# Down projection: residual additions and stores by pairs of tiles, and the last tile's in two halves on two queues

## The chip, the cores and the metric

The kernel runs on one core of one Trainium2 chip. The metric is the device time of one execution in microseconds (us), as the median over several runs; it holds everything from the launch on the core to its end. A profile is taken of one further execution: its span goes from the first to the last instruction, its own device time is a little longer. PE is TensorE (PEld its weight loads), DVE is VectorE, ACT ScalarE, POOL GpSimd, SP SyncE; a "q" behind the name means the engine's instruction queue, which issues transfers (DMA) and waits.

## The reference, cut to what matters

The input is 4 x 512 tokens of 512 features. A layer norm is followed by two branches, a long convolution of the S4 kind and a gated feed-forward layer whose weights are stored as 4-bit codes with scales; both are added to the input.

```python
x = L0_attn_u                                   # (4, 512, 512)
xn = _layernorm(x, axis=-1)
x = x + _L0_attn_ref(xn, ...) + _L0_ffn_ref(xn, ...)

def _L0_ffn_ref(x, gate_q, gate_absmax, up_q, up_absmax, down_q, down_absmax):
    Wg = dequant_nf4(gate_q, gate_absmax, (M, HD))   # M = 1792, HD = 512
    Wu = dequant_nf4(up_q, up_absmax, (M, HD))
    Wd = dequant_nf4(down_q, down_absmax, (HD, M))
    g = jnp.einsum('bsh,mh->bsm', x, Wg)
    u = jnp.einsum('bsh,mh->bsm', x, Wu)
    h = jax.nn.silu(g) * u
    return jnp.einsum('bsm,hm->bsh', h, Wd)
```

The change touches the last step: the product of `h` with `Wd` (called Down here), and the addition of `x` plus the convolution's result to it.

## The kernel before

The 2048 tokens are worked on as four blocks (`tb` = 0 to 3) of 512, each block as four tiles (`j` = 0 to 3) of 128 tokens. The 1792 hidden features are 14 tiles of 128, or 7 pairs (`p`). Every product runs in fp32r in three passes ("parts"): each operand is split into three tensors, and three matmuls replace one.

There are four stages. First a head, whose order is written out by hand (`HEAD`) and fixed for ACT, DVE, PE and SP; it normalises and transposes the input and computes the first hidden tiles. Then the hidden tiles follow one by one (`hidden`, L472): PE multiplies (L449), ACT takes the silu (L465), DVE multiplies by the up product (L469) and SP stores `h` to device memory (L470). Between them lie the S4 kernel's computation and, for each block, the convolution (`conv`, L479 to L494), which adds `x` and stores the sum `xr` to `res_dram`. Last comes Down, one block after the other (`down`, L497 to L522), from 360 us on.

In Down, for each block:

- Two PSUM tiles of two banks each, `pj[0]` and `pj[1]`, hold the four tiles' sums in blocks 0 to 2 (`po[0]` and `po[1]` are the two banks of `pj[0]`). In block 3 each of the four sums has a two-bank tile of its own and uses the first bank (L500). PSUM holds four such two-bank tiles in all (`bufs=4`), so blocks 0 and 2 use the same two, block 1 the other two, and block 3 all four.
- POOL's queue loads the residual sum into `xr` (L505; the trace calls this tile `xo`). There are two such buffers, so a block's load waits until the stores of two blocks before have left the buffer.
- For each pair `p`, SP loads `h` (L508, tile `hr`, three buffers), ACT and DVE split it into three parts (L143, L145, L147; tile `hp`, four buffers), and PE runs for each tile `j` six matmuls (two hidden tiles times three parts) of 512 columns (L514): 24 for a pair, 168 for a block, 672 in all. The down weights stay in `wdt`.
- After a tile's last matmul (`p` = 6), DVE adds the PSUM sum times a constant to the residual, in place in `xr` (L521), and SP stores the tile's 128 rows of 512 numbers to `out` (L522), 256 KB each.

Outside the head a scheduler of the framework sets the order on each engine: it takes instructions in the order in which they were written, but lets a later one go ahead of one that would have to wait by its own reckoning. The framework also sets all semaphores. It tells apart which part of a tile in SBUF an instruction reads or writes; the trace of before shows that this doesn't always hold for the two banks of a PSUM tile. Each transfer issued by SP or ACT takes the next of eight completion counters, and at the very end SP waits on all of these in a fixed order, before a barrier of all engines closes the program.

Of the kernel before, what the change touches and what calls it, by code (L numbers as in the profile page):

```python
# [12 lines left out]
ALU = mybir.AluOpType  # L13
# [3 lines left out]
P = 128  # L17
NTOK = 2048
HD = 512
# [3 lines left out]
NTB = NTOK // 512  # L23
# [3 lines left out]
NPR = NMT // 2  # L27
# [23 lines left out]
OUT = LAM + 1.0  # L51
# [45 lines left out]
def layernorm_s4_nf4_glu_kernel(  # L97
# [17 lines left out]
    nc = tc.nc  # L115
    V, S, G, T = nc.vector, nc.scalar, nc.gpsimd, nc.tensor
# [5 lines left out]
    def bank2(name):  # L122
        return psum.tile([P, 2, 512], F32, tag="ps", name=name)
# [16 lines left out]
    def split(dst, src, ks=range(3)):  # L140
        for k in ks:
            if k == 0:
                S.activation(dst[0], src, AF.Copy, scale=TRIM)  # L143
            elif k == 1:
                V.tensor_tensor(dst[1], src, f(dst[0]), ALU.subtract)  # L145
            else:
                V.scalar_tensor_tensor(dst[2], f(dst[1]), -LAM, f(dst[0]), ALU.mult, ALU.add)  # L147
# [13 lines left out]
    def rows(ap, tb):  # L161
        return ap[bass.ts(tb, 512), :].rearrange("(j p) h -> p j h", p=P)
# [331 lines left out]
        nc.sync.dma_start(res_dram[tb], xr)  # L494


    def down(tb, wd):  # L497

        if tb == NTB - 1:
            po = [bank2(f"po{tb}_{j}")[:, 0, :] for j in range(4)]  # L500
        else:
            pj = [bank2(f"po{tb}_{jj}") for jj in range(2)]
            po = [pj[j // 2][:, j % 2, :] for j in range(4)]
        xr = work.tile([P, 4, HD], F32, tag="xt", name=f"xo{tb}")
        nc.gpsimd.dma_start(xr, res_dram[tb])  # L505
        for p in range(NPR):
            hr = work.tile([P, 2, 512], F32, tag="q", name=f"hr{tb}_{p}", bufs=3)
            nc.sync.dma_start(hr, h_dram[tb][p])  # L508
            hp = work.tile([P, 3, 2, 512], F32R, tag="wp", name=f"hp{tb}_{p}", bufs=4)
            split([hp[:, i, :, :] for i in range(3)], hr)  # L510
            for j in range(4):
                for k in range(2):
                    for part in range(3):
                        T.matmul(  # L514
                            po[j], hp[:, part, k, bass.ts(j, P)], wd(p, part, k),
                            start=(p == 0 and k == 0 and part == 0),
                            stop=(p == NPR - 1 and k == 1 and part == 2),
                        )
                if p == NPR - 1:
                    o = xr[:, j, :]  # L520
                    V.scalar_tensor_tensor(o, po[j], OUT, o, ALU.mult, ALU.add)  # L521
                    nc.sync.dma_start(out[bass.ts(4 * tb + j, P), :], o)  # L522

    gu = lambda m: (("g", m), ("u", m))
    dd = lambda p: (("d", 2 * p), ("d", 2 * p + 1))
# [111 lines left out]
    for m in range(2, NMT - 2):  # L637
# [3 lines left out]
        p = {2: 0, 4: 1, 5: 2, 7: 3, 8: 4, 10: 5, 11: 6}.get(m)  # L641
# [31 lines left out]
    def wd(p, part, k):  # L673
        s = 6 * p + 2 * part + k
        return wdt[s // 4][:, s % 4, :]

    for tb in range(NTB):
        down(tb, wd)
# [65 lines left out]
```

## Time and profile before

| What | us |
| --- | --- |
| device time, median of 3 runs (lowest, highest) | 519.51 (519.39, 519.62) |
| device time of the profiled execution | 519.46 |
| its span | 517.7 |
| PE busy in the span | 510.5 |
| first matmul of Down | 360.63 |
| last addition (L521) starts | 513.70 |
| last store issued, time to landing | 514.42, 2.0 |
| mean duration of an addition of L521 (16 of them) | 0.688 |
| mean duration of the pair addition of L493 (8 of them) | 1.219 |

How to read it: the chain of work that ended last runs almost only through PE, at a granted clock of 1.00. What is not on PE at a given moment costs time only if PE waits for it, or if it lies behind the last matmul. Four windows of the Down stage, one for each block, show PE busy for 38.6, 38.2, 38.3 and 38.0 us of 38.6, 38.2, 38.3 and 38.0, DVE for 19.6, 19.6, 19.6 and 12.6, and ACT for 7.9, 7.4, 7.4 and 4.2.

### The profile page before, as it was taken

Reading aid. Unit: us, or ns where it says so; the run is one execution under the profiler, and the core shown is the slowest. Engines: PE = TensorE matmul, PEld = TensorE weight load, DVE = VectorE, ACT = ScalarE, POOL = GpSimd, SP = SyncE. Lnnn points to the kernel's source line nnn. Section 1 sums busy time; section 2 is a strip of 40 time slices with the busy share of each in tenths; the row PEclk is TensorE's granted clock in tenths of the full one; section 3 lists DMA queues with packets and bytes.
Section 4 is the critical chain, followed back from the end, with each engine's and each line's share of the span. In section 5 each row is a group of like instructions: output and inputs, shape, how many; then the busy total and the mean of one; then the engine's idle time right before and its main releaser. Section 6 shows DMA issues by size and latency. Waiting matters only on the chain.

```text
span 517.7 us, 6206 instructions
## 1 busy us (share of the span) xinstructions
PE 510.5 (99%) x2369; PEld 426.9 (82%) x2369; DVE 260.3 (50%) x352; ACT 261.6 (51%) x326; POOL 22.1 (4%) x42
## 2 busy tenths in 40 slices
PE   8999999999999999999999999999999999999996
PEld 7788888888888888888888888888888888888885
DVE  5899759935546553543522323113536536436412
ACT  7897369689999989899252202002112121121100
POOL 1310000200000000000000000121000000000000
PEclk9999999999999999999999999999999999999999
DMA  8915322796786678765845222789534524524102
GB/s 284 291 64 159 118 90 87 292 258 239 262 286 223 213 267 314 235 210 198 292 161 200 85 103 81 262 327 349 204 118 143 197 109 160 198 90 162 42 0 81
DMA packets 37085, 96.45 MB, mean 186 GB/s; under 512 B 4672, under 2 KB 5312, under 8 KB 34240
## 3 DMA queue, kind: packets, MB, share of 16 engines
q1 hardware_dynamic: 34320, 80.60, 44.9%
q0 software_dynamic: 2592, 15.21, 8.2%
q8 instruction: 18, 0.29, 0.2%
q10 hardware_dynamic: 144, 0.26, 0.1%
q14 instruction: 11, 0.09, 0.1%
HBM read 61.97 MB, written 34.08 MB: 186 GB/s over the span
## 4 chain that ended last, share of the span: by engine, by line
PE 96%; DMA 2%; SPq 1%; DVE 0%; issue 0%
PE gu L449 57%; PE po L514 30%; PE pc L487 6%; PE gu L457 2%; DMA sc_g1u<-in_gate_s_dram 2%; PE pt L204 1%; SPq L171 1%; PE pm L421 1%; SPq L250 0%; SPq L243 0%; PE pss L355 0%; DVE xo L521 0%; DVE x L192 0%
## 5 line engine op out<-in xcount | busy, mean ns | idle before, releaser
L514 PE MATMUL po<-wdt,hp 128*128 128x512 f32 x672 | 153.0, 390 | 0.0
L514 PEld LDWEIGHTS po<-wdt,hp 128*128 128x128 f32 x672 | 125.9, 188 | 27.0 <-DVE xo L521 0.9
L469 DVE SCALAR_TENSOR_TENSOR h<-gu,h 128x512 f32<-128x512 f32 x56 | 38.4, 688 | 109.4 <-ACT h L465 101.0
L143 ACT ACTIVATE hp<-hr 128x1024 fp32r<-128x1024 f32 x28 | 29.7, 1060 | 105.2 <-PE po L514 101.3
L465 ACT ACTIVATE h<-gu 128x512 f32<-128x512 f32 x56 | 33.0, 589 | 95.0 <-PE gu L449 95.0
L145 DVE TENSOR_TENSOR hp<-hr,hp 128x1024 fp32r<-128x1024 f32 x28 | 34.3, 1225 | 62.7 <-ACT hp L143 62.7
L147 DVE SCALAR_TENSOR_TENSOR hp<-hp 128x1024 fp32r<-128x1024 f32 x28 | 34.2, 1223 | 0.9
L449 PE MATMUL gu<-xhT,wp_gu 128*128 128x512 f32 x80 | 21.0, 394 | 0.0
L449 PE MATMUL gu<-xlT,wp_gu 128*128 128x512 f32 x80 | 20.7, 389 | 0.0
L487 PE MATMUL pc<-tp,xeT 128*128 128x512 f32 (+1 forms) x64 | 20.7, 323 | 0.0
L487 PE MATMUL pc<-tp,xlT 128*128 128x512 f32 (+1 forms) x64 | 20.6, 322 | 0.0
L449 PE MATMUL gu<-xeT,wp_gu 128*128 128x512 f32 x80 | 20.5, 390 | 0.0
L487 PE MATMUL pc<-tp,xhT 128*128 128x512 f32 (+1 forms) x64 | 20.3, 318 | 0.0
L521 DVE SCALAR_TENSOR_TENSOR xo<-po,xo 128x512 f32<-128x512 f32 x16 | 10.8, 688 | 18.1 <-PE po L514 18.1
L449 PEld LDWEIGHTS gu<-xlT,wp_gu 128*128 128x128 f32 x80 | 15.0, 188 | 3.1
L449 PEld LDWEIGHTS gu<-xhT,wp_gu 128*128 128x128 f32 x80 | 14.9, 188 | 3.2 <-ACT h L465 0.2
L449 PEld LDWEIGHTS gu<-xeT,wp_gu 128*128 128x128 f32 x80 | 14.9, 188 | 3.1
L457 PE MATMUL gu<-xf,q_g0u 128*128 128x256 f32 x64 | 14.6, 382 | 0.0
L457 PEld LDWEIGHTS gu<-xf,q_g0u 128*128 128x128 f32 x64 | 11.7, 190 | 1.8 <-DVE q_g0u L599 0.2
L487 PEld LDWEIGHTS pc<-tp,xhT 128*128 128x128 f32 x64 | 12.2, 190 | 0.9
L487 PEld LDWEIGHTS pc<-tp,xlT 128*128 128x128 f32 x64 | 12.0, 188 | 0.8
L487 PEld LDWEIGHTS pc<-tp,xeT 128*128 128x128 f32 x64 | 12.1, 188 | 0.6
(271 smaller groups left out, 912.1 us busy)
## 6 DMA issues: line engine op xcount, KB each, us to landing
hd<-h SPq DMA_DIRECT2D x56, 256.0 KB, 2.9
hr<-hd SPq DMA_DIRECT2D x28, 512.0 KB, 3.3
wdt<-wdd POOLq DMA_DIRECT2D x7, 1024.0 KB, 6.8
xr<-in_x_dram SPq DMA_DIRECT2D x4, 1024.0 KB, 6.8
rd<-xr SPq DMA_DIRECT2D x4, 1024.0 KB, 5.8
xo<-rd POOLq DMA_DIRECT2D x4, 1024.0 KB, 5.9
out_dram<-xo SPq DMA_DIRECT2D x16, 256.0 KB, 3.5
wdt<-wdd POOLq DMA_DIRECT2D x7, 512.0 KB, 7.3
```

Source lines behind the costliest of these rows:

```text
L143: S.activation(dst[0], src, AF.Copy, scale=TRIM)
L145: V.tensor_tensor(dst[1], src, f(dst[0]), ALU.subtract)
L147: V.scalar_tensor_tensor(dst[2], f(dst[1]), -LAM, f(dst[0]), ALU.mult, ALU.add)
L171: nc.sync.dma_start(xs[tb][:, j : j + step, :], rows(x, tb)[:, j : j + step, :])
L204: T.transpose(pt[:, i, bass.ts(c, P)], xs[tb][:, jj + i, bass.ts(c, P)], ident)
L449: T.matmul(ps[:, k, :], wp[:, part, k, bass.ts(c, P)], xT[tb][part][:, :, c, :], start=(part == 0 and c == 0), stop=(part == 2 and c == NC ...
L457: T.matmul(ps[:, k, j.start * P : j.stop * P], w[:, k, bass.ts(c, P)], xf[tb].rearrange("p j (c q) -> p j c q", c=NC)[:, j, c, :], start=( ...
L465: S.activation(h, pg, AF.Silu, scale=unit)
L469: V.scalar_tensor_tensor(h, pu, unit, h, ALU.mult, ALU.mult)
L487: T.matmul(po[:, k, i * P : HD], xT[tb][part][:, jj + k, i, :], toep[:, part, 0 : HD - i * P], start=(i == 0 and part == 0), stop=(i == NC ...
L514: T.matmul(po[j], hp[:, part, k, bass.ts(j, P)], wd(p, part, k), start=(p == 0 and k == 0 and part == 0), stop=(p == NPR - 1 and k == 1 an ...
L521: V.scalar_tensor_tensor(o, po[j], OUT, o, ALU.mult, ALU.add)
```

## The change

In blocks 0 to 2 the additions and stores of a block leave the loop over `p` and stand behind it, two in place of four: each addition reads both banks of `pj[jj]` and writes two tiles of `xr` (1024 columns), each store writes two tiles (512 KB) of `out`. In block 3 the additions stay where they are, one for each tile; only that of tile 3 is cut into two halves of 256 columns, each with a store of its own, the first issued by SP and the second by ACT. What is computed stays the same.

```diff
+    ALL = slice(0, HD)
+    HALVES = (slice(0, HD // 2), slice(HD // 2, HD))
+
     def down(tb, wd):
...
-                if p == NPR - 1:
-                    o = xr[:, j, :]
-                    V.scalar_tensor_tensor(o, po[j], OUT, o, ALU.mult, ALU.add)
-                    nc.sync.dma_start(out[bass.ts(4 * tb + j, P), :], o)
+                if p == NPR - 1 and tb == NTB - 1:
+
+                    for i, cs in enumerate(HALVES if j == 3 else (ALL,)):
+                        o = xr[:, j, cs]
+                        V.scalar_tensor_tensor(o, po[j][:, cs], OUT, o, ALU.mult, ALU.add)
+                        (nc.scalar if i else nc.sync).dma_start(out[bass.ts(4 * tb + j, P), cs], o)
+        if tb < NTB - 1:
+            for jj in range(2):
+                o = xr[:, 2 * jj : 2 * jj + 2, :]
+                V.scalar_tensor_tensor(o, pj[jj], OUT, o, ALU.mult, ALU.add)
+                nc.sync.dma_start(rows(out, tb)[:, 2 * jj : 2 * jj + 2, :], o)
```

`rows(out, tb)` is the block's 512 rows as a view of 128 partitions x 4 tiles x 512 columns.

## The prediction

> **What bounds the kernel now.** I read the chain that ended last first, then the waits of the down stage, then the timeline of one block boundary and of the last microseconds. The chain says what sets the end:
>
> ```profile
> PE 510.5 (99%) x2369; PEld 426.9 (82%) x2369; DVE 260.3 (50%) x352; ACT 261.6 (51%) x326; POOL 22.1 (4%) x42
> ...
> PE 96%; DMA 2%; SPq 1%; DVE 0%; issue 0%
> PE gu L449 57%; PE po L514 30%; PE pc L487 6%; PE gu L457 2%; DMA sc_g1u<-in_gate_s_dram 2%; PE pt L204 1%; SPq L171 1%; PE pm L421 1%; SPq L250 0%; SPq L243 0%; PE pss L355 0%; DVE xo L521 0%; DVE x L192 0%
> ```
>
> Matmuls follow each other without a gap from the start to 513.7 us; after them comes one addition (L521) and then a store. So the change can give time in two places only: in gaps between the matmuls of L514, and behind the last matmul. Gaps first, in the waits of the weight loads from 360 us on (engine and line, waited for, us in total, times, longest):
>
> ```profile
> PEld po L514 <- DVE xo L521: 0.9, 3, 0.3
> ```
>
> Three waits of 0.31 us, one at each end of blocks 0 to 2, on the very addition that the change rewrites. The timeline of the end of block 0 (start, us):
>
> ```profile
> 394.62 1.22 DVE L145 TENSOR_TENSOR hp<-hr,hp 128x1024 fp32r<-128x1024 f32 x1 [2.96 <-ACT hp L143]
> 395.76 1.28 DVE L521 SCALAR_TENSOR_TENSOR xo<-po,xo 128x512 f32<-128x512 f32 x2
> 396.50 37.95 PEld L514 LDWEIGHTS po<-wdt,hp 128*128 128x128 f32 x168 [0.31 <-DVE xo L521]
> 396.96 1.21 DVE L147 SCALAR_TENSOR_TENSOR hp<-hp 128x1024 fp32r<-128x1024 f32 x1
> 399.55 0.69 DVE L521 SCALAR_TENSOR_TENSOR xo<-po,xo 128x512 f32<-128x512 f32 x1 [0.67 <-PE po L514]
> ```
>
> The first addition ends at 396.44 and the weight load goes at 396.50: PE waits until the addition of tile 0 has read its bank before it writes tile 1, which lies in the other bank of the same two-bank tile. The addition itself was late because DVE was still in L145. Last, the end (the third line is the group of stores in that window, its last figure the time to landing):
>
> ```profile
> 513.70 0.69 DVE L521 SCALAR_TENSOR_TENSOR xo<-po,xo 128x512 f32<-128x512 f32 x1 [0.67 <-PE po L514]
> 514.42 0.33 SPq L522 DMA_DIRECT2D out_dram<-xo  x1
> out_dram<-xo SPq DMA_DIRECT2D x2, 256.0 KB, 2.0
> ```
>
> The store lands at 516.40. Then SP's records show seven steps (six waits on completion counters and a drain) 0.062 us apart up to 516.84, and the closing barrier up to 517.67. The profiled run took 519.46 us, so 1.8 us lie outside the span; the median of the runs is 519.51. I work against 519.46.
>
> **Pairs at the end of blocks 0 to 2.** *Removed*: 12 additions of 0.69 us and 12 stores of 256 KB. *Added*: 6 additions of the form 128x1024 and 6 stores of 512 KB. *Moved*: they are written after all matmuls of the block, so no addition reads a two-bank tile before that tile's last matmul is issued. The wait of 0.31 us then has nothing to wait for. What it costs PE is less than 0.31, since a queue of issued matmuls covers part. Matmuls of L514 start 0.2267 us apart; around the wait of block 0 seven starts lie 0.276, 0.337, 0.236, 0.228, 0.233, 0.230 and 0.227 apart, 0.18 more than seven times 0.2267. All 671 distances together exceed 671 x 0.2267 by 0.54, that is 3 x 0.18, with no other excess. So this part gives **-0.54 us**: all of it if the wait goes, nothing if another one of the same length comes.
>
> The cost of the new additions is hidden under PE. The row nearest to them is the same operation on a two-bank tile, on line 493:
>
> ```profile
> L493 DVE SCALAR_TENSOR_TENSOR xr<-pc,xr 128x1024 f32<-128x1024 f32 x8 | 9.7, 1219 | 3.4 <-PE pc L487 3.4
> ```
>
> 2 x 1.22 = 2.44 us a block in place of 4 x 0.69 = 2.76, while DVE is busy 19.6 of 38.2 us of a block. The second pair cannot start before the block's last matmul has ended, 0.16 us after the next block's first matmul starts (a matmul takes 0.39). Counted from that first matmul, the addition runs from 0.19 to 1.41. Behind it on DVE is L145 of a later hidden pair: it now starts at 399.7, which ACT's L143 sets in either form; that pair is needed some three periods of 5.44 us later. Blocks 1 and 2 write other buffers. Only in block 3, which takes four two-bank tiles, does PE wait for banks of block 2: tile 2 is first written 12 x 0.2267 = 2.7 us in, tile 3 after 18 x 0.2267 = 4.1. Cover of 1.3 us even if the later addition frees the bank of tile 2. On SP the first pair's store leaves at about 398.3 in place of 396.5 and 397.1, the second at about 400.8 in place of 400.3; the load of hr queued behind went at 401.94 and waited for L145 until then, so it loses at most 0.1 us, with 10 us to spare. POOL's load of xo two blocks later waits for these stores (44.1 us idle before it) but is used some 70 us later. Stores of twice the size move the same bytes in the same 2 KB packets. All of this costs **0**.
>
> **The last tile in halves.** *Addition*: one of 0.69 us becomes two on 256 columns. Two 128x256 operations back to back are in the trace, from SBUF:
>
> ```profile
> 17.12 0.75 DVE L599 TENSOR_TENSOR q_g0u<-q_g0u,sc_g0u 128x256 f32<-128x256 f32 x2
> ```
>
> So the second half ends 0.75 after 513.70 and not 0.69: **+0.06** (ends: 0, and +0.14 if the two did not overlap: 2 x 0.416). [...] The row above shows the second one starting before the first has ended, 0.75 for both.
>
> *Queue*: the second half's store is issued by ACT, idle since 493.1, the end of its last L143. The only transfer that ACT issues here stands at the start:
>
> ```profile
> 0.79 0.41 ACTq L243 DMA_DIRECT2D q_g0u<-in_gate_q_dram  x1
> ```
>
> Its first packet comes 1.34 us after issue, that of SP's first load, issued at the same moment, 1.02 after. SP's last store needed 0.83. So ACT's extra lies between 0 and 0.32; since in the tail the two issues no longer coincide (514.15 on SP for 0.33, 514.48 on ACT), I take **+0.07**, near the lower end.
>
> *Bytes*: the second half's packets are 1 KB. Packets of 1 KB took 46 ns in the load of line 402, those of 2 KB in the last store 84; each of 16 engines carries 8: 8 x 38 = **-0.30**. Other end: 84 ns each and the second half behind the first on the same engines. Then 16 x 84 = 1.34 from the first half's first packet at 514.15 + 0.83 = 514.99, against data that went from 515.25 for 8 x 84: +0.40 for store and addition together.
>
> *Closing waits*: SP waits on eight completion counters in a fixed order, and each transfer takes the next one. The last store now uses the second; five transfers fewer (12 out, 7 in) put it on the fifth. Of the seven steps behind it four remain: 3 x 0.062 = **-0.18**. Ends: 0 and -0.43.
>
> **Sum:** -0.54 + 0.06 + 0.07 - 0.30 - 0.18 = -0.89, so 519.46 - 0.89 = **518.57 us**. The ends of the unknown terms make its own range 518.3 to 518.9.
>
> **The rivals.**
> 1. *The tail gives more*: ACT issues as fast as SP (0 in place of +0.07) and SP's closing waits all pass before the last landing: -0.54 + 0.06 - 0.30 - 0.43 = -1.21, **518.25**. For it: the waits' order at the end is the compiler's. Against it: counting gives the fifth counter.
> 2. *The tail gives nothing*: writes of 1 KB cost as much as those of 2 KB: -0.54 + 0.40 - 0.18 = -0.32, **519.14**. For it: the 46 ns are from reads of device memory. The same time, -0.35 and **519.11**, comes if instead the pairs only exchange one wait of 0.3 us for another, that is, the change doesn't do what it says in blocks 0 to 2.
> 3. *The other side*: the second half's addition has to wait until the first half's store has read the same tile xo. Place: DVE at 514.1. The first store leaves at 514.15 and lands 2.0 - 0.3 = 1.7 later; the second addition then ends at about 516.3, its store lands at 518.1 and not 516.40: +1.7. Sum -0.54 + 1.7 - 0.18 = +0.98, **520.44**. It decides as soon as that wait is longer than 0.9 us. For it: PE does wait for a neighbouring bank of one tile today. Against it: in block 3 the additions at 510.98 and 512.34 write xo while the store issued 0.64 us before them is still in flight, so parts of xo are told apart.
> 4. *The banks of block 3*: if DVE takes the next hidden pair's L145 and L147 ahead of the second addition of block 2, that addition ends 4.9 us into block 3, against 4.1 when tile 3 is due: +0.8, -0.89 + 0.8, **519.37**. Against it: today the fourth addition goes ahead of L145.
>
> **How the numbers follow.** Chances: forecast 0.56, rival 1 0.19, rival 2 0.12 (both forms), rival 3 0.09, rival 4 0.04. The bound of what a measurement of this kernel can tell from no change is about 0.2%, 1.04 us, so 518.42 and 520.50. The forecast lies 0.15 inside it; some 0.3 of its chance falls below 518.42, with nearly all of rival 1: faster 0.35. Rival 3 lies at the upper edge; I give most of it, and what I may have overlooked of that kind, to slower: 0.10. Within 0.2%: 0.55. The range, 518.2 to 519.6, takes in the forecast, rivals 2 and 4 and most of rival 1, and leaves out rival 3 and the far side of rival 1. Without rivals of the other sign it would be 518.3 to 518.9.
>
> **What would show it.** Right: no wait of PEld on line 521's successor in blocks 0 to 2; the distances of L514's matmuls equal to 0.227 throughout and the L514 stretch 0.5 us shorter; six additions of 1.22 us; two of about 0.42 at the end, 0.34 apart; packets of 1 KB at 46 ns; three closing waits and a drain behind the last landing. Wrong: a PEld wait in block 3 on the pair addition (rival 4), a DVE wait on a DMA ahead of the last addition (rival 3), 84 ns for 1 KB (rival 2), or a first packet of ACT's store over 1 us after its issue.

## The result, and the profile after

The changed kernel takes 518.47 us, the median of 11 runs (518.08 to 519.55), against 519.51 for the kernel before (median of 11 runs beside them, 519.01 to 520.45). The ratio is 0.998, with a 95% interval of 0.9972 to 0.9989: a gain of 0.2%, at the edge of what such a measurement can tell. The forecast was 518.57.

The single parts are far smaller than the scatter of the times, so they are read from the profiled executions. Theirs took 519.46 (before) and 518.29 (after). The page of the changed kernel, busy time and the chain that ended last:

```profile
PE 510.2 (99%) x2369; PEld 427.9 (83%) x2369; DVE 259.6 (50%) x347; ACT 261.5 (51%) x326; POOL 22.1 (4%) x42
...
PE 96%; SPq 2%; DMA 1%; DVE 0%; issue 0%; DVEq 0%
```

PE still sets the end. Down is now line 517 (matmuls), 531 (pair additions) and 526 (additions of block 3). The groups of instructions from 360 us on (busy time, mean ns of one | idle before, with releaser):

```profile
L517 PE MATMUL po<-wdt,hp 128*128 128x512 f32 x672 | 152.5, 389 | 0.0
L517 PEld LDWEIGHTS po<-wdt,hp 128*128 128x128 f32 x672 | 126.2, 188 | 26.2
...
L531 DVE SCALAR_TENSOR_TENSOR xo<-po,xo 128x1024 f32<-128x1024 f32 x6 | 7.3, 1220 | 2.0 <-PE po L517 2.0
L526 DVE SCALAR_TENSOR_TENSOR xo<-po,xo 128x512 f32<-128x512 f32 x3 | 2.1, 692 | 15.4 <-PE po L517 15.4
...
L526 DVE SCALAR_TENSOR_TENSOR xo<-po,xo 128x256 f32<-128x256 f32 x2 | 0.8, 420 | 0.7 <-PE po L517 0.7
```

The same two groups of the kernel before:

```profile
L514 PE MATMUL po<-wdt,hp 128*128 128x512 f32 x672 | 153.0, 390 | 0.0
L514 PEld LDWEIGHTS po<-wdt,hp 128*128 128x128 f32 x672 | 125.9, 188 | 27.0 <-DVE xo L521 0.9
```

The weight loads name no releaser any more: the three waits on the addition are gone. Matmul busy time fell from 153.0 to 152.5. DVE at the end of block 0, from the timeline:

```profile
394.33 1.23 DVE L145 TENSOR_TENSOR hp<-hr,hp 128x1024 fp32r<-128x1024 f32 x1 [2.96 <-ACT hp L143]
395.59 1.22 DVE L147 SCALAR_TENSOR_TENSOR hp<-hp 128x1024 fp32r<-128x1024 f32 x1
396.74 1.22 DVE L531 SCALAR_TENSOR_TENSOR xo<-po,xo 128x1024 f32<-128x1024 f32 x1
398.63 1.23 DVE L531 SCALAR_TENSOR_TENSOR xo<-po,xo 128x1024 f32<-128x1024 f32 x1 [0.68 <-PE po L517]
399.78 1.23 DVE L145 TENSOR_TENSOR hp<-hr,hp 128x1024 fp32r<-128x1024 f32 x1
```

The first pair addition runs after L147, at a time when nobody waits for it. And the end of the kernel, timeline and groups of stores (the last figure of these is the time to landing):

```profile
512.87 0.76 DVE L526 SCALAR_TENSOR_TENSOR xo<-po,xo 128x256 f32<-128x256 f32 x2 [0.67 <-PE po L517]
513.66 0.35 ACTq L527 DMA_DIRECT2D out_dram<-xo  x1
...
out_dram<-xo SPq DMA_DIRECT2D x1, 128.0 KB, 1.7
out_dram<-xo ACTq DMA_DIRECT2D x1, 128.0 KB, 1.7
```

One addition of 0.69 became two of 0.76 together, and the landing comes 1.7 us after issue and not 2.0.

The spans differ by 1.1 us, which is more than the change did. The first matmul of Down starts at 360.63 before and at 360.35 after; over these and the nine profiled executions of the experiments it lies anywhere between 360.23 and 361.33. The scatter arises in the head: the 17th matmul of line 457, before which PE has waited for the normalisation of the second part of the input, comes at 18.19 before, at 17.95 after, and between 17.83 and 18.95 over all; from there to the first Down matmul it is 342.39 to 342.46 us in every one. So I split each profiled execution into four pieces: up to the first Down matmul (which the change doesn't touch), from the first to the last start of Down's 672 matmuls, from there to the last landing, and from there to the end of the span. The last column is the device time less the start of the first Down matmul, against 158.83 for the kernel before.

| Kernel | device time | first Down matmul | matmul starts span | to the landing | to the end | without the head, against before |
| --- | --- | --- | --- | --- | --- | --- |
| before | 519.46 | 360.63 | 152.64 | 3.12 | 1.28 | 0 |
| after | 518.29 | 360.35 | 152.09 | 2.94 | 1.19 | -0.89 |
| pairs alone | 519.22 | 361.06 | 152.09 | 3.14 | 1.14 | -0.67 |
| halves alone | 519.54 | 360.81 | 152.73 | 2.98 | 1.31 | -0.10 |
| own PSUM tiles | 519.40 | 361.11 | 152.09 | 3.11 | 1.27 | -0.54 |
| both halves on SP | 518.76 | 360.70 | 152.09 | 3.06 | 1.09 | -0.77 |
| late single additions | 518.65 | 360.55 | 152.09 | 2.98 | 1.32 | -0.73 |
| split on POOL | 520.44 | 361.33 | 152.92 | 3.12 | 1.28 | +0.28 |
| queues exchanged | 518.92 | 360.96 | 152.09 | 2.94 | 1.20 | -0.87 |
| queues exchanged, eighth counter | 518.00 | 360.23 | 152.09 | 2.93 | 1.01 | -1.06 |
| ACT's store 4 us earlier | 519.29 | 361.24 | 152.09 | 3.05 | 1.20 | -0.78 |

(All in us, each row from one execution. The four pieces of a row add up to its span. The rest of the device time lies outside the span: 1.70 to 1.74 us in the six kernels in which ACT issues a store near the end, namely after, halves alone, late single additions, both with queues exchanged, and the last row, and 1.79 to 1.82 in the other five.)

### The profile page after: what moved, and what is told of

The parts are those of the page before. It is cut to its first block, busy times and chain, and to the rows that moved or that the text cites. A ratio compares the mean times of both kernels' runs of the same rounds, so it can differ in the third digit from the quotient of the medians.

```text
span 516.6 us, 6194 instructions
## 1 busy us (share of the span) xinstructions
PE 510.2 (99%) x2369; PEld 427.9 (83%) x2369; DVE 259.6 (50%) x347; ACT 261.5 (51%) x326; POOL 22.1 (4%) x42
## 4 chain that ended last, share of the span: by engine, by line
PE 96%; SPq 2%; DMA 1%; DVE 0%; issue 0%; DVEq 0%
PE gu L449 57%; PE po L517 29%; PE pc L487 6%; PE gu L457 2%; DMA q_g1u<-in_up_q_dram 1%; PE pt L204 1%; SPq L171 1%; SPq L250 1%; PE pm L421 1%; SPq L243 0%; PE pss L355 0%; DVE x L192 0%; DVE xo L526 0%; DVEq L750 0%
## 5 line engine op out<-in xcount | busy, mean ns | idle before, releaser
L517 PE MATMUL po<-wdt,hp 128*128 128x512 f32 x672 | 152.5, 389 | 0.0
L145 DVE TENSOR_TENSOR hp<-hr,hp 128x1024 fp32r<-128x1024 f32 x28 | 34.3, 1225 | 62.7 <-ACT hp L143 62.7
L147 DVE SCALAR_TENSOR_TENSOR hp<-hp 128x1024 fp32r<-128x1024 f32 x28 | 34.3, 1224 | 1.0
L181 DVE BATCH_NORM_STATS2 st<-x 128x6 f32<-128x512 f32 x16 | 10.8, 675 | 3.3 <-DMA x<-in_x_dram 3.2
```

The costliest lines, as they stand in the source:

```text
L181: V.bn_stats(st[:, j, :], xs[tb][:, j, :])
L517: T.matmul(po[j], hp[:, part, k, bass.ts(j, P)], wd(p, part, k), start=(p == 0 and k == 0 and part == 0), stop=(p == NPR - 1 and k == 1 an ...
```

## The experiments

My theory: the pairs take away three waits of PE, 0.54 us in all, and the end gives some 0.3, of which 0.18 only by the place of the last store among the completion counters; to that place the pairs' fewer stores contribute too. The main rival: the wait only moves, and the gain is the tail's.

**Each part alone.** The pairs of blocks 0 to 2 with block 3 as before:

```diff
-                    for i, cs in enumerate(HALVES if j == 3 else (ALL,)):
+                    for i, cs in enumerate((ALL,)):
```

> The pairs of blocks 0 to 2 alone; block 3 adds and stores its four tiles whole, as before the change. Theory (the two parts of the change add up, the pairs remove the three waits of PE): the starts of the 672 Down matmuls span 152.09 us and not 152.64, no weight load waits for an addition; last matmul start to last landing as before, 3.12; the last store takes the fourth completion counter, so five closing steps remain behind it in place of seven, -0.12. Sum against before: -0.54 - 0.12 = -0.66. Rival (the pairs only move the wait, the change's gain comes from the tail): the span of the matmul starts stays at 152.6.

Measured: starts over 152.09 us, no wait of a weight load on an addition, landing after 3.14, to the end 1.14, together -0.67. By time the ratio to before is 0.9986 (0.9977 to 0.9995). The theory holds; the rival falls.

The halves, with blocks 0 to 2 as before (the additions in the loop, one for each tile; the last one cut as in the change):

```diff
                 if p == NPR - 1:
-                    o = xr[:, j, :]
...
+                    last = tb == NTB - 1 and j == 3
+                    for i, cs in enumerate(HALVES if last else (ALL,)):
+                        o = xr[:, j, cs]
...
+                        (nc.scalar if i else nc.sync).dma_start(out[bass.ts(4 * tb + j, P), cs], o)
```

> The halves of the last tile on two queues alone; blocks 0 to 2 as before the change. Theory: the starts of the 672 Down matmuls span 152.64 us as before, with three waits of 0.31; last matmul start to last landing 2.94 as in the changed kernel (before 3.12); the last store takes the third counter, six closing steps behind it, -0.06; ACT's part in the closing barrier 0.12 later, as in the changed kernel. Sum: -0.18 - 0.06 + 0.12 = -0.12. Rival (the tail is the larger part): -0.5 or more from last matmul start to the end of the span.

Measured: -0.10, ratio 0.9999 (0.999 to 1.0008). The waits of the weight loads in Down of this kernel (us in total, times, longest):

```profile
PEld po L517 <- DVE xo L526: 0.9, 3, 0.3
```

They are back, as expected. The two parts add up: -0.67 and -0.10 against -0.89 together. The 0.12 over lies in this execution's matmul starts (152.73 against 152.64) and in landings that came 0.02 to 0.04 later.

**What makes PE wait.** Is it the two sums in one PSUM tile, or DVE's lateness? In the kernel before, each sum gets a PSUM tile of its own in every block; the 16 single additions stay where they were:

```diff
-        if tb == NTB - 1:
-            po = [bank2(f"po{tb}_{j}")[:, 0, :] for j in range(4)]
-        else:
-            pj = [bank2(f"po{tb}_{jj}") for jj in range(2)]
-            po = [pj[j // 2][:, j % 2, :] for j in range(4)]
+        po = [bank2(f"po{tb}_{j}")[:, 0, :] for j in range(4)]
```

> The kernel before, with one edit: in every block each of the four sums has a two-bank PSUM tile of its own, as block 3 has; 16 single additions and 16 stores in the loop as before. Theory (PE waited because two sums shared one PSUM tile, so that the neighbour's addition had to end first): no weight load waits for an addition, the matmul starts span 152.09 us, -0.54 against before, although DVE does exactly the same additions at the same places. Rival A (the wait comes from DVE being late with single additions, whatever tile they read): three waits of about 0.3 stay, 152.6. Rival B (block n+1 now takes over the banks of block n, so PE waits there): a wait at tile 3 of each next block, if the addition of tile 3 ends more than 4.1 us into it.

Measured: -0.54, all of it in the matmul starts. The weight loads in this kernel, and DVE at the end of block 0:

```profile
L510 PEld LDWEIGHTS po<-wdt,hp 128*128 128x128 f32 x672 | 126.2, 188 | 26.1
```

```profile
395.09 1.23 DVE L145 TENSOR_TENSOR hp<-hr,hp 128x1024 fp32r<-128x1024 f32 x1 [2.96 <-ACT hp L143]
396.23 1.28 DVE L517 SCALAR_TENSOR_TENSOR xo<-po,xo 128x512 f32<-128x512 f32 x2
397.43 1.22 DVE L147 SCALAR_TENSOR_TENSOR hp<-hp 128x1024 fp32r<-128x1024 f32 x1
```

DVE does what it did before, in the same order and just as late behind L145, and no weight load waits. (PE's order did change: the two matmuls of the next block that stood ahead of the end of block 0 now come behind it.) Neither rival shows: a bank taken over from the block before was free in time. The times alone could not have told this (ratio 0.9992, 0.9983 to 1.0001).

The other half of the question: does the wait go if the addition comes on time? In the kernel before, POOL takes the split operations that stood in DVE's way:

```diff
-            split([hp[:, i, :, :] for i in range(3)], hr)
+            ps = [hp[:, i, :, :] for i in range(3)]
+            split(ps, hr, (0,))
+            if p == 2 and tb > 0:
+                G.tensor_tensor(ps[1], hr, f(ps[0]), ALU.subtract)
+                G.tensor_scalar(ps[2], f(ps[1]), -LAM, None, ALU.mult)
+                G.tensor_tensor(ps[2], f(ps[2]), f(ps[0]), ALU.add)
+            else:
+                split(ps, hr, (1, 2))
```

> The kernel before, with POOL in place of DVE for the two split operations of the hidden pair whose split falls on the end of the previous block (pair 2 of blocks 1 to 3), as three operations on POOL; additions and stores as before. Theory (the wait needs two things: a shared PSUM tile and an addition that DVE starts late, because it is in L145): the first addition starts within 0.1 us of its tile's last matmul, PE's waits fall from 0.31 to under 0.1 each, and the matmul starts span 152.1 to 152.3. Rival (the shared tile alone makes the wait, whatever DVE is doing): three waits of about 0.3, 152.6. A loss elsewhere would show if POOL's three operations take more than the 15 us they have.

A miss. The waits of the weight loads, and then the first addition and the loads around it in the timeline:

```profile
PEld po L521 <- DVE xo L528: 1.5, 6, 0.3
```

```profile
395.53 0.69 DVE L528 SCALAR_TENSOR_TENSOR xo<-po,xo 128x512 f32<-128x512 f32 x1 [3.17 <-PE po L521]
```

```profile
395.34 0.64 PEld L521 LDWEIGHTS po<-wdt,hp 128*128 128x128 f32 x3
396.28 2.86 PEld L521 LDWEIGHTS po<-wdt,hp 128*128 128x128 f32 x13 [0.30 <-DVE xo L528]
399.33 0.76 PEld L521 LDWEIGHTS po<-wdt,hp 128*128 128x128 f32 x4 [0.19 <-DVE xo L528]
```

The addition started 0.04 after its tile's last matmul had ended (that one started at 395.11 and took 0.39), and PE waited all the same, now twice a block, with the matmul starts spread over 152.92 in this one execution. The scheduler had changed PE's order too: it put only four matmuls of another tile between the two sums of the shared tile, where it had put six and two more before (why it did so is not shown; it may have reckoned with an early addition). The waiting weight load could have gone at about 396.02, and the addition ended at 396.22.

So the edit changed two things at once, and what DVE's lateness alone costs is not tested. The trace of before allows an estimate: there tile 0's last matmul ended at 394.80, so an addition of 0.69 in time would have been over by about 395.5, 0.7 ahead of the weight load's turn at 396.22; it ended at 396.44. By this estimate the wait took both in that order, a shared tile and a late addition. With four matmuls in between, the shared tile makes PE wait for an addition that is in time. What all the waits have in common is the shared tile. That their length hangs on how much other work stands between its two sums is an estimate from these two orders (before, 0.31 us with eight matmuls between and a late addition; here 0.30 for the first, with four and an addition in time); no run varies that work alone.

**Place or pairing.** The changed kernel, with single additions and stores behind the loop:

```diff
-            for jj in range(2):
-                o = xr[:, 2 * jj : 2 * jj + 2, :]
-                V.scalar_tensor_tensor(o, pj[jj], OUT, o, ALU.mult, ALU.add)
-                nc.sync.dma_start(rows(out, tb)[:, 2 * jj : 2 * jj + 2, :], o)
+            for j in range(4):
+                o = xr[:, j, :]
+                V.scalar_tensor_tensor(o, po[j], OUT, o, ALU.mult, ALU.add)
+                nc.sync.dma_start(out[bass.ts(4 * tb + j, P), :], o)
```

> The changed kernel, with four single additions and four single stores behind the loop in blocks 0 to 2 in place of two pairs. Theory (it is the place that counts: an addition written after the block's matmuls can hold up none of them): no weight load waits for an addition, matmul starts of Down span 152.09 us as with pairs; the last store takes the third counter, six closing steps, 0.12 more than with pairs. Rival (the pairing counts, since it frees DVE): the three waits come back, 152.6.

Measured in one execution: 152.09, no wait; to the end 1.32 against 1.19, that is 0.13 for the two further closing steps. For PE's waits it is the place that counts.

**The second queue.** The changed kernel with both halves on SP:

```diff
-                        (nc.scalar if i else nc.sync).dma_start(out[bass.ts(4 * tb + j, P), cs], o)
+                        nc.sync.dma_start(out[bass.ts(4 * tb + j, P), cs], o)
```

> The changed kernel, with the second half's store issued by SP too. Theory (the two queues share the 16 engines, so the second queue saves only SP's issue time): the second issue starts 0.38 after the first, at +0.05 against ACT's; its first packet comes 0.84 after issue in place of ACT's 0.88; landing within 0.05 of the changed kernel's; and ACT's late drain in the closing barrier goes, -0.12 from there. Sum against the changed kernel: -0.15 to 0. Rival (the second queue makes the halves' stores go at the same time and is what shortens the tail): landing at least 0.2 later.

Half a miss. The landing came 0.12 later than in the changed kernel, not within 0.05, and short of the rival's 0.2. SP's second issue started 0.10 later than ACT's had; SP was still issuing the first one. So 0.10 of the landing's 0.12 lies in the issue. And ACT's late drain was gone, 1.09 against 1.19. Inside the span, then, the second queue gives 0.12 and takes 0.10. The device time doesn't show the 0.10: outside the span a kernel with a late store on ACT is some 0.08 shorter (1.70 to 1.74 against 1.79 to 1.82, see the table; means over 11 or more runs of a kernel give 1.71 to 1.72 against 1.79 to 1.82). Without the head the second queue is worth its whole 0.12, -0.89 against -0.77. Where these 0.08 lie is open. The time's ratio to before, 0.999 (0.9981 to 0.9999), doesn't separate it from the changed kernel's.

With the queues exchanged (ACT the first half, SP the second):

```diff
-                        (nc.scalar if i else nc.sync).dma_start(...)
+                        (nc.scalar if j == 3 and i == 0 else nc.sync).dma_start(...)
```

> The changed kernel, with the queues of the two halves exchanged: ACT stores the first half, SP the second. Theory (SP was busy issuing the first half when the second was ready, and ACT's own start is 0.05 slower; ACT's late drain at the end costs 0.10 however early it issued): SP's issue starts 0.03 after the second addition, the landing comes 2.89 to 2.94 after the last matmul's start, and the time from landing to the end stays 1.19. Rival (ACT's drain is late because it had issued the last store a short time before): the time from landing to the end falls to 1.09, the whole tail from 4.13 to about 4.0.

The end of this kernel in the timeline:

```profile
513.48 0.75 DVE L526 SCALAR_TENSOR_TENSOR xo<-po,xo 128x256 f32<-128x256 f32 x2 [0.67 <-PE po L517]
513.94 0.35 ACTq L527 DMA_DIRECT2D out_dram<-xo  x1
514.26 0.33 SPq L527 DMA_DIRECT2D out_dram<-xo  x1
```

SP issues 0.03 after the second addition's end (514.23). The landing 2.94, the time behind it 1.20: the theory's numbers, though no better than the change itself (ratio to before 0.9982, 0.9973 to 0.9991). That ACT issued 0.3 us earlier changed nothing about its drain. So I put ACT's only late store 4 us earlier, at tile 0 of block 3, and both halves on SP:

```diff
-                        (nc.scalar if i else nc.sync).dma_start(...)
+                        (nc.scalar if j == 0 else nc.sync).dma_start(...)
```

> The changed kernel with both halves' stores on SP, and the store of block 3's first tile, 4 us earlier, on ACT. Theory (ACT's drain at the end is late because ACT issued one of its last instructions as a transfer just before; 0.33 us earlier was not enough, 4 us is): landing to the end 1.09 as with everything on SP. Rival (any transfer that ACT issues after its last activation makes its drain late, whenever): 1.19. The rest as with both halves on SP: matmul starts 152.09, last landing 3.06 after the last matmul's start, 0.12 more than in the changed kernel.

ACT's store in the timeline:

```profile
510.40 0.35 ACTq L527 DMA_DIRECT2D out_dram<-xo  x1
```

The last landing came at 516.39, six us later. Measured in one execution: 1.20 again. The theory falls, the rival holds: a store that ACT issues after its last activation costs 0.10 in the closing barrier, six us before the last landing as well as two. In the records ACT's drain there starts 0.35 after its release and takes 0.14, against 0.08 and 0.01 in the kernel before; it is the last of the engines' drains to end, and the barrier goes on 0.03 behind it. Why is open. In device time it comes back here too: -0.78 without the head, against -0.77 with both halves on SP.

**The closing counters.** Queues exchanged, and three pair stores of blocks 0 and 1 cut in two, so that the last store takes the last of the eight counters:

```diff
-                nc.sync.dma_start(rows(out, tb)[:, 2 * jj : 2 * jj + 2, :], o)
+                step = 1 if 2 * tb + jj < 3 else 2
+                for j in range(0, 2, step):
+                    nc.sync.dma_start(
+                        rows(out, tb)[:, 2 * jj + j : 2 * jj + j + step, :], o[:, j : j + step, :]
+                    )
```

> The exchanged queues, and three of the pair stores of blocks 0 and 1 cut into two stores of one tile each, so that the last store takes the eighth and last of the completion counters that SP waits on at the end. Theory (each counter that comes after the last store's in that list costs 0.062 once the store has landed): landing to SP's drain 0.07 in place of 0.26, the whole tail 0.18 shorter than with the queues exchanged alone, about 3.95 or, without ACT's late drain, 3.8; matmul starts still 152.09. Rival (the steps are hidden behind another part of the closing barrier): the time from landing to the end stays where it is.

Landing to SP's drain took 0.08 in place of 0.26, landing to the end 1.01 in place of 1.20: the theory holds, and the rival falls. This is the shortest version by its pieces, 0.17 below the change. The times cannot show that: ratio to before 0.998 (0.9971 to 0.9988), the same as the change's.

## Why the prediction was right, point by point

- *Block ends*: -0.54 forecast, -0.55 measured (152.64 to 152.09), and the same 152.09 in the run with own tiles, which takes away the shared tile and leaves DVE's work in its place. The new additions cost nothing, as reckoned: 1.22 each, under PE, and block 3 waited for no bank. A slip without effect: I put the second pair's store at 400.8, and it went at 399.89. Beside the head (0.28) and the wait (0.18) I had forgotten that two matmuls of the next block, 0.45, had stood ahead of the end of block 0 and now come behind it. Two more slips without effect: the L145 that the prediction puts at 399.7 stands at 400.69 in the timeline of before; and PE does wait after the start, 0.95 us for DVE up to 17.26, in the head, which the change leaves alone.
- *Two additions for one*: +0.06 forecast, +0.06 measured (last matmul start to end of addition 1.118 to 1.181). The second half starts 0.34 after the first; a half took 0.420 by its row, the two together 0.76.
- *ACT's start*: +0.07 forecast, +0.05 measured: first packet 0.88 after issue, against 0.84 on SP. The 0.32 of the start of the kernel did not come back.
- *Packets of 1 KB*: -0.30 forecast, -0.31 measured. Stores of 1 KB took 46 ns a packet, like the loads; the data went for 0.49 us (514.54 to 515.03) in place of 0.79. This settles rival 2's first form; the matmul starts settle its second.
- *Closing waits*: -0.18 forecast and -0.19 found between landing and SP's drain (0.45 to 0.26). But the span ended only 0.09 sooner, since the barrier now waited for ACT's drain, 0.10. That term was missing from the sum; the runs with everything on SP and with ACT's store 4 us earlier show that it comes with a late store on ACT. Missing too was that the time outside the span falls by 0.07 to 0.08 in the same kernels. That the two nearly cancel was not foreseen; it is luck.
- *Sum*: -0.89 forecast. Inside the span the pieces give -0.55 - 0.18 - 0.09 = -0.82, and the time outside the span was 0.07 shorter: -0.89. The remaining 0.28 of the profiled difference is the head's scatter. The medians differ by 1.04, by the ratio's interval 0.6 to 1.5; that the median came within 0.10 of the forecast is luck as well. The pieces bear the forecast out, not the median.
- *Rivals*: 3 (the second half waits for the first half's store) did not come: the two additions lie 0.34 apart, and no transfer stands between them. 4 did not come either. 1 had one true point, that more closing steps can be saved, but not in this change.

The step that carried the forecast was to read what three waits cost from the distances of the matmul starts (0.18 each) and not from the waits' own 0.31.

## What to carry to other kernels

Where a framework sets the semaphores, a PSUM tile of several banks can tie its banks together: here one bank was read while matmuls into the next were still to come, and PE waited for the reader three times, 0.31 us each, even though the banks differ. Read such a tile after its last matmul, or give each sum its own: either took all three waits away here, with the matmul starts over 152.09 us in place of 152.64. What a wait costs a busy engine is read from the distances of its starts (0.18 us here), not from the waiting time shown (0.31); and parts of some 0.1 us are read from pieces of profiled executions that share no scatter, since times of whole runs hide them. The profile's span is not the device time: what is lost at the end of the one can come back outside it (here 0.10 lost, some 0.08 back), so compare both.

## What the runs showed of the hardware

- A store issued by ACT after its last activation made the closing barrier 0.10 us longer through ACT's drain, in six of six such kernels, issued 2 or 6 us before the last landing: 0.92 to 0.93 from SP's drain to the end of the span, against 0.81 to 0.83 in the five without one. The device time outside the span is shorter by nearly as much in the same six, 1.70 to 1.74 against 1.79 to 1.82.
- Each completion counter that was waited on behind the last store's cost 0.06 us at the end: 0.45, 0.39, 0.32, 0.26 and 0.08 from landing to SP's drain with seven, six, five, four and one step left.
- Stores of 1 KB packets took 46 ns a packet, as the load of line 402 did, against 84 for 2 KB.
- The head, the same in all eleven kernels, ended anywhere within 1.1 us (first Down matmul at 360.23 to 361.33): the main scatter in these profiled executions.
